# Causal attention: norms of the first batch made a stage earlier, and sums over keys for four heads every second slot

## The chip, the cores and the metric

The kernel runs on one core of a Trainium2 chip. The core has a matrix engine (TensorE, PE in the profile; its weight loads are listed as PEld), a vector engine (VectorE, DVE), an activation engine (ScalarE, ACT), a general engine (GpSimd, POOL) and queues for transfers (SyncE, SP, among them). The metric is the device time of one execution in microseconds. Before the change the median of three runs is 1987.32 us (1986.11 to 1991.52).

## The reference

The program is a stack of four layers over a tensor x of 4 batches, 512 tokens and 256 features in 32-bit floats. Each layer is an attention over a context of 64 tokens (for the second layer with an exponential feature map), and then a feed-forward part. The part that matters is that of the second layer: a causal attention with 16 heads of 16 features, queries and keys and values made from a latent, and then a mixture of experts.

```python
def rmsnorm(x, w):
    norm = jnp.sqrt(jnp.mean(x * x, axis=-1, keepdims=True)) + EPS
    return x / norm * w

def mla(xn, W_kvd, W_qd, W_ku, W_qu, W_vu, W_ropeq, W_ropek, W_o):
    kv_lat = xn @ W_kvd
    q_lat = xn @ W_qd
    ...                       # k, q: a plain and a rotated half; v
    scores = jnp.einsum('bqhd,bkhd->bhqk', qq, kk) * scale
    scores = jnp.where(causal[None, None], scores, jnp.finfo(scores.dtype).min)
    probs = jax.nn.softmax(scores, axis=-1)
    y = jnp.einsum('bhqk,bkhd->bqhd', probs, v).reshape(B, S, H)
    return y @ W_o
...
# the second layer
x = x + _L1_xattn_ref(ctx_1024, ctx_1024, _layernorm(x), ...)
x = _layernorm(x)             # inside the call of _L1_ffn_ref
x = x + mla(rmsnorm(x, w_ln1), ...)
x = x + moe(rmsnorm(x, w_ln2), ...)
```

So the causal attention of a batch starts with two norms of the same rows, one after the other: a layer norm, whose result is also the residual, and a root-mean-square norm.

## The kernel before

Tokens stand in blocks of 128 on the partitions; a batch is four such blocks. The stages that the change touches follow one another: the attention over the context of the second layer (`xattn`, in the profile from about 571 to 701 us), and the causal attention (`mla`, 701 to 1168). The mixture of experts comes after.

*The attention over the context* runs over four batches. For each it makes the queries of the next batch in between (the generator `new`, asked for a step by `some(new, n)` at five places), exponentials on ScalarE (`cpr`, L563), their sums over keys on TensorE (`ps_den`, L572), a reciprocal on VectorE (`crs`, L581), a broadcast of it (`ps_bc`, L591), the sums with the values (`ps_cy`, L597) and a projection (`ps_p`, L612). For the last batch `new` is empty.

*The causal attention* begins with `mla_heads` of batch 0, straight through: the layer norm into `xl` (ScalarE, L345), the squares (ScalarE, L354), a square root (L362), the multiplication into `xn` (VectorE, L368), transposes to `xnT` (TensorE, L377; copied out by VectorE, L381), and then the latent (`ps_lat`, L1180) and for each of four token blocks queries, values and keys (`ps_mq`, `ps_mv`, `ps_mk`), with copies on ScalarE (L1195, L1213), rotations on VectorE (L1186) and sums on GpSimd (L1196).

Then comes a loop over slots t = 0 to 140, with 128 slots of scores: four batches, four groups of four heads, four blocks of 128 queries or keys, two pairs of heads. Slot t does in TensorE's order:

- the scores of one pair of heads for the maximum (`ps_ms`, L1235), for 128 queries against all keys so far;
- the scores of the pair of slot t-11 for the weights (`ps_mx`, L1250), for 128 keys against all later queries, with the negative maximum as an extra feature. ScalarE takes the exponential (L1252) and GpSimd masks the diagonal block (L1254);
- the causal mask added to the first scores (L1238), which VectorE then reduces to the maximum (L1240);
- `behind(1)`: one piece of `mla_after` of the previous batch. These are, for each of four blocks, transposes of the sums (`ps_mn`), transposes back (`ps_myT`) and the projection (`ps_mw`), with VectorE's reciprocal, product and addition between them (L1310 for the addition); then the second norm and its transposes, the router (`ps_r`), the top two, the ranks (`ps_rank`), scatters of the rows on GpSimd's queue (`xs`, L859, eight a batch), and a shared expert (`ps_sg`, `ps_su`, `ps_sd`);
- the sums over keys of the pair of slot t-13 (`mla_sum`, `ps_mo`, L1273), 32 columns of the matrix engine for a head;
- in odd slots, `next(new)`: a piece of `mla_heads` of the next batch;
- when t%8 is 5, the transposes of queries and keys for the next group of heads (`mla_turned`, L1220); when t%8 is 2, at the start of the slot, those of the queries with their maxima.

TensorE takes its instructions in the order written (`in_order(PE)`); for the other engines a scheduler sets the order. In PSUM, the first scores have one buffer (`s1`, two banks for a pair of heads), so have the second (`s2`), and so has the output of the sums (`po`). The exponentials have four buffers (`mpr`). So the first scores of the next slot wait until VectorE has reduced those of this one.

```python
            behind(1)
            if last:
                self.mla_sum(pool, sts[last[0]], *last[1:], made.pop(last))
            ...
            if t % 2:
                next(new, None)
```

Of the kernel before, what the change touches and what calls it, by code (L numbers as in the profile page):

```python
# [11 lines left out]
F32 = mybir.dt.float32  # L12
# [10 lines left out]
P = 128  # L23
B, S, E = 4, 512, 256
# [164 lines left out]
class Net:  # L189
# [165 lines left out]
        return ss  # L355

    def rmsnorm(self, x, out):

        nc = self.nc
        ss = self.sumsq(x)  # L360
        nr = self.sm("rms_n", [P, GT])
        nc.scalar.activation(nr, ss, AF.Sqrt, scale=1.0 / E)  # L362
        ne = self.sm("rms_e", [P, GT])
        nc.vector.tensor_scalar(ne, nr, 1e-5, None, ALU.add)
        rs = self.sm("rms_r", [P, GT])
        nc.vector.reciprocal(rs, ne)
        for i in range(GT):
            nc.vector.tensor_scalar(out[:, i], x[:, i], rs[:, i : i + 1], None, ALU.mult)  # L368
# [265 lines left out]
        st.va = values(pool, g)  # L634
        yield

    def xattn(self, query, values, scale, dv, W, bias, before=None, after=None, keys=None, begin=lambda: None):

        with self.room("xattn") as pool, self.banks(mm=4, sc=1), ExitStack() as stack:
            mxs = [pool.tile([P, 4, 32], F32, tag=f"mx{i}", name=f"mx{i}", bufs=1) for i in range(GT)]
            for m in mxs:
                self.nc.gpsimd.memset(m, 0.0)
            for t in range(NT if before else 0):
                before.load(pool, t, self.nc.scalar if t // GT == 1 else self.nc.sync, bufs=12)
            stack.enter_context(self.in_order(PE))
            if keys:
                for _ in self.ctx_ready(pool, keys):  # L650
                    pass
            sts = [SimpleNamespace(g=g, pr=[]) for g in range(B)]
# [12 lines left out]

            nf = NH * dv // P
            old = late = iter(())
            new = heads(0)  # L670
            first = ExitStack()
            first.enter_context(self.in_order(ACT, DVE, POOL) if before else nullcontext())
            some(new)
            for st in sts:
                if st.g:
                    old = rest(sts[st.g - 1])
                new = heads(st.g + 1) if st.g + 1 < B else iter(())

# [24 lines left out]
            for _ in old:  # L703
                some(late, 1)
            some(late)
# [434 lines left out]
class Layers(Net):  # L1140


    def route(self, moe, g, rw, fine=False):
# [17 lines left out]

        return (whole for whole in steps() if whole or fine)

    def mla_heads(self, pool, g, st):


        nc = self.nc
        xl = st.xl = self.tail.tile([P, GT, E], F32, tag="xl", name="xl", bufs=3)
        self.layernorm(g, xl)
        yield  # L1170
        xr = self.xn_tile()
        self.rmsnorm(xl, xr)
# [89 lines left out]
        )  # L1262
        return pr

    def mla_sum(self, pool, st, o, j, h, pr):

        nc = self.nc
        if j == 0 and h == 0:
            st.po = self.po.tile([P, S], F32, name="ps_mo")
        for r in range(2):  # L1270
            n = 2 * h + r
            at = (4 * o + n) * (HD + 1)
            nc.tensor.matmul(  # L1273
                st.po[32 * n : 32 * n + 32, j * P :],
                st.va[:, j, at : at + 32],
                pr[:, r, : S - j * P],
                start=(j == 0),
                stop=(j == GT - 1),
                tile_position=(0, 32 * n),
            )  # L1280
# [57 lines left out]
        yield from moe.add(g, rows, *picked)  # L1338
        yield from self.shared_expert(pool, g, xT, sgu, sd)

    def mla(self, pool, short, tail, moe, sgu, sd, soon):

        nc = self.nc
        sts = [SimpleNamespace(qT={}, kT={}, qm={}, ys=[]) for _ in range(B)]
        for g, st in enumerate(sts):
            if g < 2:
                st.q, st.k = (  # L1350
                    (pool if g else short).tile([P, GT, NH, 32], F32, tag=f"m{n}{g}", name=f"m{n}{g}", bufs=1) for n in "qk"
# [33 lines left out]
        for t in range(32 * B + 13):  # L1385
# [27 lines left out]
            behind(1)  # L1413
        return old[0]

    def l1_ffn(self):
        nc, d = self.nc, self.d
        moe = Routed(self, 7, E, d["e1gu"], d["e1d"], "e1", STAMP, w=V_LN2)
        with ExitStack() as stack:
# [23 lines left out]
                moe.begin(stack.enter_context(self.room("l1h", side="right")))  # L1443

            with self.in_order(PE):
                last = self.mla(pool, short, tail, moe, sgu, sd, soon)
# [262 lines left out]
    def run(self):  # L1709
# [4 lines left out]

        W1, W3 = [], []
        moe = Routed(self, 8, 704, d["e0gu"], d["e0d"], "e0", 2 * STAMP)
        with ExitStack() as stack:
            with self.room("l0h") as held:
                with self.room("l0w", 1) as keep:
# [5 lines left out]
                with self.room("l0b", side="right") as pool, banks():  # L1725
# [8 lines left out]

                    with self.in_order(DVE, SP):
                        moe.blocks(pool, self.route(moe, B - 1, self.rw0, fine=True), other=later())
            self.xattn(
                self.query_features, self.values_features, 1.0 / 16.0, 2 * HD, W1[0], R_FCB, before=moe
            )
        moe = self.l1_ffn()  # L1740
        with banks():
            self.l2(moe)
        moe = Routed(self, 8, 512, d["e3gu"], d["e3d"], "e3", 0)
# [36 lines left out]
```

## Time and profile before

| what | us |
|---|---|
| median of the runs | 1987.32 (1986.11 to 1991.52) |
| the profiled execution's own time | 1997.2 |
| its span | 1995.5 |
| TensorE busy | 1712.2 (86%) |
| VectorE busy | 1020.4 (51%) |
| ScalarE busy | 671.4 (34%) |
| GpSimd busy | 424.3 (21%) |
| sums over keys, `ps_mo` L1273, 512 instructions | 97.1 |
| first scores, `ps_ms` L1235, 512 instructions | 111.7 |
| reductions, `mq` L1240, 128 instructions | 105.7 |
| first to last start of the first scores | 732.5 to 1133.2 |

A line of the timeline gives the start, the duration, the engine, the line of the kernel, the operation, the tiles (out <- in), the shape and the number of instructions put together, and in brackets how long the engine was idle before and what ended that. Of stretches, a line gives the length, the busy time of TensorE, its weight loads, VectorE, ScalarE and GpSimd with their number of instructions, the granted clock of TensorE as a share of full speed, the share of the transfer engines and the rate. A matrix product in 32-bit floats is two instructions in the profile, so the sum over keys of two heads shows as "x4".

### The profile page before, as it was taken

To read this page: it belongs to the slowest core of one execution; us is meant where nothing else is said; L and a number is where in the kernel's file an instruction comes from. 1 tells how busy PE (TensorE), PEld (TensorE's weight loads), DVE (VectorE), ACT (ScalarE), POOL (GpSimd) and SP (SyncE) were. 2 spreads that over 40 slices of the span, in tenths; PEclk is the share of its full clock that TensorE was granted. 3 is DMA by queue.
4 is the path that set the end of the run, shared out by engine and by line. 5 is a ranking of instruction groups with operands and counts; after the bars stand their busy time and mean duration, and the time that the engine had idled before them with its cause. 6 is when DMAs were issued, how large, how long until landed. Compare 5 with 4: busy or idle time off the path is not lost.

```text
span 1995.5 us, 25928 instructions
## 1 busy us (share of the span) xinstructions
PE 1712.2 (86%) x8752; PEld 970.5 (49%) x8752; DVE 1020.4 (51%) x3011; ACT 671.4 (34%) x1254; POOL 424.3 (21%) x594
## 2 busy tenths in 40 slices
PE   5878999999789868898989888985998887899993
PEld 2435666666444433343433344543665443455552
DVE  3655544444454343444454536546989565553333
ACT  3333222222254323335343432233445334222220
POOL 2031211111240021123131312223113103221112
PEclk8989999999899968998999999995899898999997
DMA  9528787887400100000001035972000001788884
GB/s 294 160 84 330 273 294 281 290 287 281 134 1 1 39 1 1 1 1 22 1 27 42 19 101 173 298 254 85 1 1 1 12 1 65 238 293 301 298 298 162
DMA packets 109350, 271.61 MB, mean 136 GB/s; under 512 B 13409, under 2 KB 71201, under 8 KB 99105
## 3 DMA queue, kind: packets, MB, share of 16 engines
q1 hardware_dynamic: 82976, 227.97, 33.9%
q0 software_dynamic: 10176, 28.00, 3.7%
q10 hardware_dynamic: 16064, 13.98, 2.1%
q8 instruction: 70, 1.15, 0.2%
q14 instruction: 64, 0.52, 0.1%
HBM read 220.48 MB, written 49.42 MB: 135 GB/s over the span
## 4 chain that ended last, share of the span: by engine, by line
PE 69%; DVE 18%; ACT 6%; issue 3%; DMA 2%; POOL 1%; SPq 0%; ACTq 0%; DVEq 0%; POOLq 0%
PE ps_gu L1030 20%; PE ps_de L1072 10%; PE ps_ms L1235 4%; PE ps_mo L1273 3%; DVE mq L1240 2%; PE ps_p L612 2%; PE ps_mx L1250 2%; PE ps_f L1633 2%; PE ps_xT L377 2%; PE ps_he L1059 2%; PE ps_bc L591 2%; ACT cpr L563 2%; PE ps_cx L557 1%; PE ps_ms L1238 1%; PE ps_cy L597 1%
## 5 line engine op out<-in xcount | busy, mean ns | idle before, releaser
L1030 PE MATMUL ps_gu<-e_wgu,e_xT 128*128 128x352 f32 (+1 forms) x1088 | 420.9, 526 | 13.1 <-DVE e_xT L1022 5.8
L1030 PEld LDWEIGHTS ps_gu<-e_wgu,e_xT 128*128 128x128 f32 x1088 | 195.5, 190 | 155.7 <-issue 71.4
L1072 PE MATMUL ps_de<-e_wd,e_hT 128*128 128x256 f32 x932 | 233.0, 387 | 10.8 <-ACT e_hT L303 3.1
L1075 POOL DMA_INDIRECT ys<-e_y,e_to x116 | 113.2, 976 | 482.6 <-ACT e_y L1074 336.5
L1072 PEld LDWEIGHTS ps_de<-e_wd,e_hT 128*128 128x128 f32 x932 | 172.8, 191 | 83.6 <-issue 39.0
L1047 DVE TENSOR_TENSOR e_h<-e_s,ps_gu 128x352 f32<-128x352 f32 (+2 forms) x155 | 83.4, 538 | 244.8 <-PE ps_gu L1030 185.0
L1240 DVE TENSOR_REDUCE mq<-ps_ms 128x2 f32<-128x256 f32 (+3 forms) x128 | 105.7, 826 | 139.9 <-PE ps_ms L1238 136.6
L1046 ACT ACTIVATE e_s<-ps_gu 128x352 f32<-128x352 f32 (+2 forms) x155 | 74.1, 478 | 280.3 <-PE ps_gu L1030 264.9
L1074 ACT ACTIVATE e_y<-ps_de,e_wt 128x256 f32<-128x256 f32 x116 | 55.0, 474 | 262.6 <-PE ps_de L1072 250.0
L1252 ACT ACTIVATE mpr<-ps_mx 128x1024 f32<-128x1024 f32 (+3 forms) x128 | 90.1, 704 | 146.9 <-PE ps_mx L1250 137.9
L1235 PE MATMUL ps_ms<-mkT,mqT 32*128 32x512 f32 (+3 forms) x512 | 111.7, 515 | 25.8 <-DVE mq L1240 24.3
L859 POOL DMA_INDIRECT xs<-xn,e_at x96 | 94.5, 985 | 120.4 <-DVE e_fi L893 39.7
L1250 PE MATMUL ps_mx<-mqm,mkT 32*128 32x128 f32 (+3 forms) x512 | 107.4, 497 | 1.3 <-ACT mpr L1252 1.3
L1254 POOL TENSOR_SCALAR_AFFINE_SELECT mpr<-mpr 128x256 f32<-128x256 f32 x128 | 52.2, 409 | 250.7 <-ACT mpr L1252 250.6
L1273 PE MATMUL ps_mo<-mpr,va 128*32 128x128 f32 (+3 forms) x512 | 97.1, 461 | 4.5 <-POOL mpr L1254 3.2
L1633 PE MATMUL ps_f<-w,xqT 128*128 128x352 f32 x256 | 86.1, 478 | 1.2 <-ACT xqT L1624 1.2
L1059 PE MATMUL ps_he<-consts_sb,e_h 128*128 128x128 f32 x466 | 76.3, 277 | 9.6 <-DVE e_h L1047 6.7
L557 PE MATMUL ps_cx<-q,kbd 32*128 32x512 f32 x256 | 45.2, 806 | 44.1 <-ACT cpr L563 44.1
L1235 PEld LDWEIGHTS ps_ms<-mkT,mqT 32*128 32x128 f32 x512 | 40.9, 195 | 80.6 <-DVE mq L1240 56.0
L1019 DVE COPY e_xT<-ps_xe 128x256 f32<-128x256 f32 x78 | 33.0, 423 | 86.7 <-PE ps_xe L1016 86.7
L377 PE MATMUL ps_xT<-consts_sb,xn 128*128 128x128 f32 x256 | 48.8, 330 | 32.4 <-ACT xn L345 18.7
L1059 PEld LDWEIGHTS ps_he<-consts_sb,e_h 128*128 128x128 f32 x466 | 53.7, 138 | 29.4 <-DVE e_h L1047 13.7
(317 smaller groups left out, 2816.0 us busy)
## 6 DMA issues: line engine op xcount, KB each, us to landing
e_wgu<-in_e0gu SPq DMA_DIRECT2D x39, 1408.0 KB
e_wgu<-in_e3gu SPq DMA_DIRECT2D x39, 1024.0 KB
e_wd<-in_e0d SPq DMA_DIRECT2D x39, 768.0 KB
e_wd<-in_e3d SPq DMA_DIRECT2D x39, 512.0 KB
e_wgu<-in_e1gu SPq DMA_DIRECT2D x38, 512.0 KB
xs<-z SPq DMA_DIRECT2D x16, 1040.0 KB
e_x<-xs SPq DMA_DIRECT2D x116, 130.0 KB
e_wd<-in_e1d SPq DMA_DIRECT2D x38, 256.0 KB
```

Of the source, the lines that this page charges most:

```text
L377: nc.tensor.transpose(ps[:, i * P : (i + 1) * P], x[:, i, c * P : (c + 1) * P], self.ident)
L859: r = nc.gpsimd.indirect_dma_start(out=net.xs, out_offset=bass.IndirectOffsetOnAxis(ap=at[:, k, i : i + 1], axis=0), in_=rows[:, i], in_of ...
L1030: nc.tensor.matmul(ps[:, :n], xT[:, c], wgu[:, c, cols], start=(c == 0), stop=(c == NC - 1))
L1059: self.nc.tensor.transpose(ps[:r, f - f0], h[:, f * P : f * P + r], net.ident)
L1072: nc.tensor.matmul(po[:, :E], hT[:r, f], wd[:r, f], start=(f == 0), stop=(f == self.nf - 1))
L1075: r = nc.gpsimd.indirect_dma_start(out=net.ys, out_offset=bass.IndirectOffsetOnAxis(ap=at, axis=0), in_=y, in_offset=None)
L1235: nc.tensor.matmul(ps[:, r, :n], st.qT[o][rows, diag], st.kT[o][rows, :n], start=True, stop=False)
L1240: nc.vector.tensor_reduce(st.q[:, i, at : at + 2, HD], ps[:, :, :n], AX.X, ALU.max, negate=True)
L1250: nc.tensor.matmul(ps[:, r, :n], st.kT[o][rows, keys], st.qm[o][rows, j * P :], start=True, stop=True)
L1252: nc.scalar.activation(pr[:, :, :n], ps[:, :, :n], AF.Exp, scale=HD**-0.5)
L1273: nc.tensor.matmul(st.po[32 * n : 32 * n + 32, j * P :], st.va[:, j, at : at + 32], pr[:, r, : S - j * P], start=(j == 0), stop=(j == GT - 1),
L1633: nc.tensor.matmul(ps[:, :H], xT[:, c], w[:, c, k * H : (k + 1) * H], start=(c == 0), stop=(c == NC - 1))
```

## The change

There are two parts.

*The norms of the first batch.* The layer norm, the root-mean-square norm and the transposes become a generator of their own, `mla_normed`. For batch 0 it is given to `xattn` of the second layer as `ahead`, in place of the empty `new` of its last batch, which takes a step from it at the places where the next batch's queries would be made. `xl` of batch 0 gets a buffer that outlives the stage. For the other batches `mla_heads` starts with `mla_normed`; it has one step more than before, so that the transposes and all that follow come one odd slot later.

*The slots.* `mla_sum` sums four heads at once, in even slots only, when the second pair of a group is ready. Pieces of the previous batch (`behind`) come twice in an odd slot, one before and one after the piece of the next batch, and not in even slots.

```diff
+    def rmsnorm_steps(self, x, out):
 
         nc = self.nc
         ss = self.sumsq(x)
         nr = self.sm("rms_n", [P, GT])
         nc.scalar.activation(nr, ss, AF.Sqrt, scale=1.0 / E)
+        yield
...
-                new = heads(st.g + 1) if st.g + 1 < B else iter(())
+                new = heads(st.g + 1) if st.g + 1 < B else iter(ahead)
...
+    def mla_normed(self, g, st):
+
+        xl, xr = st.xl, self.xn_tile()
+        yield from self.layernorm_steps(g, xl)
+        yield
+        yield from self.rmsnorm_steps(xl, xr)
+        yield
+        st.xT = self.transposed(xr, V_LN1)
+        yield
+
     def mla_heads(self, pool, g, st):
 
 
         nc = self.nc
-        xl = st.xl = self.tail.tile([P, GT, E], F32, tag="xl", name="xl", bufs=3)
-        self.layernorm(g, xl)
-        yield
-        xr = self.xn_tile()
-        self.rmsnorm(xl, xr)
-        yield
-        yield
-        xT = self.transposed(xr, V_LN1)
-        yield
+        if g:
+            yield from self.mla_normed(g, st)
+        xT = st.xT
...
-    def mla_sum(self, pool, st, o, j, h, pr):
-
-        nc = self.nc
-        if j == 0 and h == 0:
+    def mla_sum(self, pool, st, o, j, prs):
+
+        nc = self.nc
+        if j == 0:
             st.po = self.po.tile([P, S], F32, name="ps_mo")
-        for r in range(2):
-            n = 2 * h + r
+        for n in range(4):
             at = (4 * o + n) * (HD + 1)
             nc.tensor.matmul(
                 st.po[32 * n : 32 * n + 32, j * P :],
                 st.va[:, j, at : at + 32],
-                pr[:, r, : S - j * P],
+                prs[n // 2][:, n % 2, : S - j * P],
                 start=(j == 0),
                 stop=(j == GT - 1),
                 tile_position=(0, 32 * n),
             )
-        if j == GT - 1 and h == 1:
+        if j == GT - 1:
...
-            behind(1)
-            if last:
-                self.mla_sum(pool, sts[last[0]], *last[1:], made.pop(last))
+
+            if t % 2:
+                behind(1)
+            if last and last[3]:
+                g, o, j, _ = last
+                self.mla_sum(pool, sts[g], o, j, [made.pop((g, o, j, h)) for h in range(2)])
...
             if t % 2:
                 next(new, None)
+                behind(1)
...
             self.xattn(
-                self.query_features, self.values_features, 1.0 / 16.0, 2 * HD, W1[0], R_FCB, before=moe
+                self.query_features, self.values_features, 1.0 / 16.0, 2 * HD, W1[0], R_FCB,
+                before=moe, ahead=self.mla_normed(0, first),
             )
```

More of the change, by code (lines that the diff above doesn't have):

```diff
@@ L357, in rmsnorm @@
     def rmsnorm(self, x, out):
+        for _ in self.rmsnorm_steps(x, out):
+            pass
+    def rmsnorm_steps(self, x, out):
         nc = self.nc
@@ L635, in ctx_heads, with xattn @@
         yield
-    def xattn(self, query, values, scale, dv, W, bias, before=None, after=None, keys=None, begin=lambda: None):
+    def xattn(self, query, values, scale, dv, W, bias, before=None, after=None, keys=None, begin=lambda: None, ahead=()):
         with self.room("xattn") as pool, self.banks(mm=4, sc=1), ExitStack() as stack:
@@ L1339, in mla_after, with mla @@
         yield from self.shared_expert(pool, g, xT, sgu, sd)
-    def mla(self, pool, short, tail, moe, sgu, sd, soon):
+    def mla(self, pool, short, tail, moe, sgu, sd, first, soon):
         nc = self.nc
         sts = [SimpleNamespace(qT={}, kT={}, qm={}, ys=[]) for _ in range(B)]
+        sts[0].xl, sts[0].xT = first.xl, first.xT
         for g, st in enumerate(sts):
+            if g:
+                st.xl = tail.tile([P, GT, E], F32, tag=f"xl{g}", name=f"xl{g}", bufs=1) if g < 3 else first.xl
             if g < 2:
@@ L1414, in mla, with l1_ffn @@
         return old[0]
-    def l1_ffn(self):
+    def l1_ffn(self, first):
         nc, d = self.nc, self.d
@@ L1445, in l1_ffn @@
             with self.in_order(PE):
-                last = self.mla(pool, short, tail, moe, sgu, sd, soon)
+                last = self.mla(pool, short, tail, moe, sgu, sd, first, soon)
             mla.close()
@@ L1716, in run @@
         moe = Routed(self, 8, 704, d["e0gu"], d["e0d"], "e0", 2 * STAMP)
+        rows = ExitStack()
         with ExitStack() as stack:
@@ L1736, in run @@
                         moe.blocks(pool, self.route(moe, B - 1, self.rw0, fine=True), other=later())
+            first = SimpleNamespace()
+            first.xl = rows.enter_context(self.room("mla_first", 1)).tile([P, GT, E], F32, tag="xl", name="xl0")
             self.xattn(
-                self.query_features, self.values_features, 1.0 / 16.0, 2 * HD, W1[0], R_FCB, before=moe
-            )
-        moe = self.l1_ffn()
+                self.query_features, self.values_features, 1.0 / 16.0, 2 * HD, W1[0], R_FCB,
+                before=moe, ahead=self.mla_normed(0, first),
+            )
+        moe = self.l1_ffn(first)
+        rows.close()
         with banks():
```

## The prediction

> **What bounds the kernel now.** The page's table of engines has TensorE (PE) busy 86% of the span and VectorE 51%; its chain of waits is 69% PE and 18% VectorE. That is an average over stages, so I went to the stages touched: the end of the attention over the context (to 700.8 us) and the causal attention (701 to 1168), first by the timeline, then by stretches with their granted clock. This is PE at the seam between them (start, duration, line, operation, in brackets the idle time before and its releaser):
>
> ```profile
> 693.59 7.17 PE L612 MATMUL ps_p<-fcT_sb,cy 128*128 128x256 f32 x32
> 704.89 0.33 PE L377 MATMUL ps_xT<-consts_sb,xn 128*128 128x128 f32 x1 [4.12 <-DVE xn L368]
> ...
> 709.64 1.12 PE L377 MATMUL ps_xT<-consts_sb,xn 128*128 128x128 f32 x4 [0.84 <-DVE xnT L381]
> 710.55 3.62 PE L1180 MATMUL ps_lat<-xnT,Wlat_sb 128*128 128x512 f32 x4
> ```
>
> PE has nothing of its own from 700.76 to 710.55 but eight transposes, each late behind a normalization. Two more stretches of the timeline matter for where the norms go: the start of the last batch of the context attention, and its last reciprocal.
>
> ```profile
> 603.83 1.28 ACT L563 ACT_TABLE_LOAD   x1
> 605.13 1.88 ACT L563 ACTIVATE cpr<-ps_cx 128x2048 f32<-128x2048 f32 x1
> 607.06 2.00 PE L557 MATMUL ps_cx<-q,kbd 32*128 32x512 f32 x16 [0.54 <-ACT cpr L563]
> 611.91 1.07 PE L572 MATMUL ps_den<-cpr,pairs_sb 128*32 128x512 f32 x8 [1.00 <-ACT cpr L563]
> ```
>
> ```profile
> 680.32 3.36 DVE L581 RECIPROCAL crs<-ps_den 128x512 f32<-128x512 f32 x1 [10.89 <-PE ps_den L572]
> 683.74 1.24 PE L591 MATMUL ps_bc<-crs,pairs_sb 128*128 128x512 f32 x2 [3.48 <-DVE crs L581]
> ```
>
> In the first, PE waits for ScalarE's exponentials; in the second, it idles 3.48 us behind VectorE. In the causal attention the timeline shows the inside of a slot:
>
> ```profile
> 1029.27 0.28 PE L1238 MATMUL ps_ms<-caus,id 128*128 128x128 bf16 x2
> 1029.48 1.05 PE L1273 MATMUL ps_mo<-mpr,va 128*32 128x512 f32 x4
> 1029.59 1.23 DVE L1240 TENSOR_REDUCE mq<-ps_ms 128x2 f32<-128x1024 f32 x1
> 1030.87 0.70 PE L1235 MATMUL ps_ms<-mkT,mqT 32*128 32x512 f32 x2 [0.33 <-DVE mq L1240]
> ```
>
> The next slot's scores wait for the reduction of this one (one double buffer of scores), whatever PE did meanwhile. So a slot lasts its scores (ms, mx), then the longer of two: the reduction, or the other work on PE, its fill. With the durations of these rows, pitch = (ms+mx) + max(0.39 + reduction, 0.21 + fill). Last, the granted clock (stretch, length, busy us of PE, PEld, DVE, ACT, POOL, then PEclk, DMA):
>
> ```profile
> 732.50:741.00 8.50, 5.84 (x26) 3.02 (x28) 2.24 (x4) 0.00 (x0) 0.00 (x0) 0.50 0.00 0
> 831.40:834.80 3.40, 2.25 (x20) 1.05 (x22) 1.78 (x3) 1.63 (x2) 0.82 (x2) 1.00 0.00 0
> 834.80:838.20 3.40, 3.40 (x15) 0.58 (x8) 1.16 (x2) 0.81 (x1) 0.41 (x1) 0.50 0.00 0
> ```
>
> A stretch with PE busy 66% is followed by one at half clock.
>
> **Part 1, the norms of the first batch.** Removed from the seam: PE starts the latents (L1180) at 700.8 instead of 710.55, 9.8 us earlier. From there to the first scores (732.55) it is 22.0 us now. The chain in it is copies, rotations and POOL's sums (first at 717.0); ScalarE's eight normalizations (0.59 each) and eight squares (0.40) of batches 1 and 2, done now at 701 to 708 while PE waits, will stand among those copies, and POOL's sums behind its memsets, which begin when the last projection ends (700.83) and run to 708.4. Against that, half clock reigns now from 705.1 to 722.2, and PE comes straight from a full stretch of projections. So the way takes 19 to 22 us; the first scores come 9.8 to 13 us earlier, taken as 12.
>
> Added in the attention over the context: PE's eight transposes (0.48 each at half clock, 1.1 to 2.1 in all) go, in PE's written order, ahead of the broadcasts at 683.74, into the 3.48 us behind the reciprocal; their two copies (0.75 each) into 3.3 us in which VectorE idles after it. Cost nil; without that cover 2.1 us. But ScalarE's part goes between the norm's square root at 603.5 and the table load at 603.83: four normalizations (2.07), four squares and their sums (1.6), a square root (0.2), and about 0.6 of waiting for VectorE's 1/sd. Behind them are queued the exponentials of 605.13, which PE awaits 0.54 us already. So up to 4.5 us go straight onto the path; the lower bound is nil, if PE's weight work or later idle (1.00 before the L572 row) absorbs it. I take 4.5, as PE's order is fixed there. No DMA or SP instruction moves: the weights of the latents are issued by 695.6 and landed by 699. Head: -12 + 4.5 = **-7.5** (-13 to -3).
>
> **Part 2, sums of four heads.** Now each slot sums two heads: 1.05 us at 512 columns (0.98 on the path), less at fewer; 0.66 in the mean, 84.8 us over 128 slots. Four heads occupy four column groups. The nearest row is the denominators' (L572 above): eight instructions in 1.07 us against four in 1.05. So the four-head sum costs 0.08 more than the two-head one; the bounds are 0 and 0.98 (no overlap, which would leave nothing gained). Half the sums, 42 us of PE work, go. What they return is much less: an even slot keeps its reduction as floor, and an odd one falls to it.
>
> By the rule, slots 0 to 127 take 370.7 us before, and the trace has 401.5: most slots agree within 0.1, and the rest is half clock in slots 0 to 9 (+9.9) and stalls (+20.9). With the written order of after the rule gives 348.0. Two slots show the working. Slot 21 (number five of its eight, zero to seven): 0.86 + 0.21 + fill (sum 0.98, values 0.75, keys 0.87, turns 1.86) = 5.53, as measured; after: 0.86 + 0.21 + (queries 0.84, turns 1.86) = 3.77. Slot 27, number three: now 1.07 + 0.39 + 0.69 = 2.15, held by the reduction; after, values and keys (1.62) fall there: 2.90. Summed by number, zero to seven: -6.3, -0.3, -8.4, +13.6, -4.8, -12.3, -3.0, -1.2. Sum **-22.6**.
>
> Paired pieces make new stalls. Pieces of the previous batch go twice in an odd slot instead of once in each, so a piece follows its predecessor at once in PE's order: the transposes of a projected block wait for VectorE's reciprocal (0.2) and product (0.45). Where queries and keys do not lie between, that is 1.3 to 1.5 (slots 45, 77, 109), 0.8 to 1.3 at 113, 115 and 119, 0.25 at 47, 51, 79, 83. In slots 57 and 89 the second norm and its transposes share a slot: the squares, the table load (1.28), the root (0.2), the multiplications (1.14) make 5 to 5.5 us against 3.2 of PE work, so +2.2 each, and +3 at 121, where nothing fills. POOL's queue: eight row scatters per batch at 1.27 us pitch now go as two, six with a causal mask (L1254) between; after as three, three, two. The mask, and with it the sum, waits 3.8 us instead of 7.6; I price this at 2.3 a batch. Sum of these: 20. Of the 20.9 of stalls now, those at the scatter of slots 99 to 101 (7.5 over the rule) go or shrink, I take 8. Net **+12** (+4 to +20).
>
> The clock: where no pieces of a previous batch are left (slots 27 to 44, 59 to 66 and 91 to 98, 34 in all) the slots numbered six and seven of eight hold 3.2 us of PE work in 5.4, 60%, below the 66% that tripped at 831.4. A stretch at half clock costs 1.0 to 1.7 us; some eight more of them make **+9**. Bounds: nil, if windows straddle busier slots; +33, if all 34 run at half, at the price of 0.96 worked out below.
>
> Here the Trainium skill speaks against the change. "TensorE: Matmul & The Clock Gate" gives, under "Why this matters for your kernels", the rule that idle gaps of more than about 3 us are what to avoid if the clock is not to drop; by that this term would be nil. Under "A second HAM failure mode: psum-queue depth-cycling" it says that frequent micro-idles between groups of matmuls throttle too, which gives no price. The trace sides with the second: the longest idle in 831.4 to 834.8 was 0.71 us.
>
> The last slots (1134 to 1168, 34 us, PE busy 31.65) hold 13 two-head sums; half is 4.3 us, of which I take **-2** (-4 to 0), because masks behind six scatters still gate them.
>
> **Sum:** -7.5 - 22.6 + 12 + 9 - 2 = -11. It is made on the profiled execution (1997.2 us, 9.9 over the median of 1987.3); on the median it gives 1976.
>
> **Rivals.** *Slower, by the clock alone.* In slots 0 to 7, at half clock and without sums, the slots took 24.8 us where the rule gives 17.1: +0.96 a slot. Without the clock term the sum is -20; it turns at 21 extra slots at half clock and passes +6 at 27. All 34 quiet slots would give +33 - 20 = +13: 2000. For: return to full needs a stretch that is nearly all busy, and from 732 to 763 it did not come. Against: fills of 2.7 us or more every eight slots, at 834.8, returned it after one window. *More gained:* the clock stays full and the new stalls are hidden by the slack of even slots: -7.5 - 22.6 + 4 - 2 = -28, 1959. For: VectorE is free when its pieces come. Against: PE's order is written, so nothing passes a waiting piece. *Nothing to tell from before:* sums were hidden behind reductions anyway, the stalls and the clock eat the slots' gain (-22.6 + 20 + 9), and the head, half lost to the copies, is left at -5: with the tail at nil that is +1: 1989.
>
> **How the numbers follow.** The forecast with its terms near these (1968 to 1981) 0.34; more gained 0.20; same 0.16; slower 0.30. Faster: 0.34 + 0.20 = 0.54. About 0.3%, 6 us, is what a measurement tells from no change. The range, 1955 to 2003, leaves out the ends of the clock rival and of all terms at their best; the forecast's own is 1968 to 1981.
>
> **What would show it.** Right: L1180's matmuls start directly after the last projection; a gap of some 4 us ahead of the exponentials near 604 to 610; slots like 21 of 3.8 us; idle before the transposes of blocks in slots 45 and 57; four-head sums of 1.1 us at 512 columns. Wrong: four-head sums near 2 us (slots give nothing); granted clock of 0.5 over whole eights; the gap at 604 absent; or the masks' wait not shortened.

## The result, and the profile after

The changed kernel takes 2011.0 us (median of four runs, 2010.1 to 2014.0), the kernel before 1986.7 beside it: 1.0124 times as long, 95% interval 1.0098 to 1.0150. It is slower by 24 us where 11 us less were forecast, and the time lies outside the range of 1955 to 2003.

The two profiled executions differ by only 12.8 us, because that of before (1997.2) was 10 us above its median. Laid over one another by TensorE's instructions, they differ as follows: +5.2 us in the experts of the first layer, which the change does not touch; -5.4 between there and the first scores of the causal attention; +20.7 in the 128 slots; -2.1 in the last slots; -5.8 later, in the third and fourth layers, which the change does not touch either. So the head and the tail did about what was forecast, and the slots did the opposite. The three stages together give +13 us; where the other 11 us of the medians' difference lie, the two profiled executions do not show.

The page after, its first table and its chain of waits:

```profile
PE 1702.5 (85%) x8752; PEld 981.5 (49%) x8752; DVE 1015.8 (51%) x3011; ACT 670.2 (33%) x1254; POOL 422.4 (21%) x594
...
PE 69%; DVE 18%; ACT 6%; issue 3%; DMA 2%; POOL 1%; SPq 0%; ACTq 0%; DVEq 0%; POOLq 0%
```

In whole-span shares nothing is to be seen. The stretches show it: slots 0 to 126, then the ten slots from 57, then the ten from 89. The first three lines are of before, the other three of after (stretch, length, then busy us of PE, PEld, DVE, ACT, POOL, the granted clock, the transfers' share and rate):

```profile
732.55:1132.71 400.16, 354.22 (x2261) 153.93 (x2261) 183.50 (x381) 155.13 (x260) 83.93 (x174) 0.93 0.04 12
899.20:932.90 33.70, 29.43 (x193) 13.27 (x191) 17.87 (x56) 20.78 (x38) 6.79 (x13) 0.85 0.01 4
1010.95:1039.08 28.13, 24.87 (x195) 12.22 (x193) 16.57 (x52) 14.35 (x23) 7.12 (x14) 1.00 0.02 5
```

```profile
732.33:1152.49 420.16, 350.33 (x2260) 164.39 (x2260) 184.60 (x381) 154.86 (x260) 83.61 (x174) 0.83 0.04 11
896.19:937.28 41.09, 34.11 (x196) 17.12 (x193) 18.56 (x57) 20.86 (x38) 8.49 (x15) 0.63 0.03 10
1011.86:1055.10 43.24, 35.39 (x198) 18.27 (x195) 19.89 (x71) 14.55 (x23) 8.59 (x16) 0.64 0.03 10
```

TensorE lost about half of its time in the sums (`ps_mo` takes 55.2 us instead of 97.1) and its busy time fell by 4 us only, because it ran slower: the mean granted clock went from 0.93 to 0.83. In the ten slots from 57 and the ten from 89 it was 0.63 and 0.64, where it had been 0.85 and 1.00. Added up over the slots, TensorE was at half clock for 54.5 us before and for 141.9 us after.

The time of groups of slots, from the first scores of one to those of the next group, in us:

| slots | before | after | what lies there |
|---|---|---|---|
| 0-10 | 33.0 | 32.2 | no sums yet |
| 11-26 | 45.1 | 40.9 | heads of the next batch |
| 27-44 | 48.0 | 50.9 | little but scores and sums |
| 45-56 | 40.7 | 39.9 | projections of batch 0 |
| 57-66 | 33.7 | 41.1 | second norm, its transposes, router |
| 67-76 | 37.4 | 34.6 | scatters, shared expert |
| 77-88 | 40.7 | 40.0 | projections of batch 1 |
| 89-98 | 28.1 | 43.3 | second norm, its transposes, router |
| 99-108 | 39.2 | 31.7 | scatters, shared expert |
| 109-120 | 34.2 | 37.0 | projections of batch 2 |
| 121-126 | 20.2 | 28.7 | second norm, its transposes, router |

The three groups with a second norm lose 31 us, all others together gain 11. TensorE's timeline at the first of them, slot 57 of after:

```profile
895.41 0.85 PE L1281 MATMUL ps_mo<-mpr,va 128*32 128x384 f32 x8
896.19 0.49 PE L1244 MATMUL ps_ms<-mkT,mqT 32*128 32x128 f32 x4
899.09 0.80 PE L1259 MATMUL ps_mx<-mqm,mkT 32*128 32x128 f32 x4 [2.42 <-ACT mpr L1261]
899.82 0.39 PE L1247 MATMUL ps_ms<-caus,id 128*128 128x128 bf16 x2
900.01 1.59 PE L1212 MATMUL ps_mq<-Wup_sb,lat 128*128 128x384 f32 x2
```

And ScalarE's over the same stretch:

```profile
895.11 0.42 ACT L354 ACTIVATE sq<-xl 128x256 f32<-128x256 f32 x1 [1.88 <-DVE xl L1318]
...
895.63 1.28 ACT L366 ACT_TABLE_LOAD   x1
896.93 0.21 ACT L366 ACTIVATE rms_n<-ss 128x4 f32<-128x4 f32 x1
897.15 1.28 ACT L1261 ACT_TABLE_LOAD   x1
898.44 0.60 ACT L1261 ACTIVATE mpr<-ps_mx 128x512 f32<-128x512 f32 x1
```

The same place in the kernel before, TensorE and ScalarE (slot 57 starts at 899.20):

```profile
898.43 0.84 PE L1273 MATMUL ps_mo<-mpr,va 128*32 128x384 f32 x4
899.83 0.38 ACT L1252 ACTIVATE mpr<-ps_mx 128x256 f32<-128x256 f32 x1 [0.32 <-POOL x L1323]
899.86 0.63 PE L1273 MATMUL ps_mo<-mpr,va 128*32 128x256 f32 x4
900.24 1.28 ACT L362 ACT_TABLE_LOAD   x1
900.41 0.91 PE L1207 MATMUL ps_mv<-Wup_sb,lat 128*128 128x384 f32 x2
901.16 1.03 PE L1210 MATMUL ps_mk<-Wrk_sb,xnT 128*128 128x256 f32 x4
```

Three things are to be read. The first line of TensorE is a sum of four heads: eight instructions over 384 columns in 0.85 us, where four took 0.84 before; the sums do overlap. Then TensorE stands still for 2.42 us: the scores for the weights have one buffer, its last contents wait for an exponential, and that stands in ScalarE's order behind the norm's square root with a table load (1.28 us) on either side of it. Before, the exponential that TensorE needed next stood ahead of the table loads (899.83 against 900.24), and TensorE had a sum, values and keys to make meanwhile. The third is what follows: the queries of slot 57 take 1.59 us, where 0.91 is usual at full clock; half clock is granted from 897.9 to 915.0. Slot 57 takes 10.1 us instead of 3.4, slot 59 7.5 instead of 2.1. (Before, the transposes stood in slot 58; slots 57 and 58 together take 12.6 us instead of 7.2.)

At the seam, TensorE after:

```profile
706.52 7.17 PE L617 MATMUL ps_p<-fcT_sb,cy 128*128 128x256 f32 x32
713.53 1.88 PE L1189 MATMUL ps_lat<-xnT,Wlat_sb 128*128 128x512 f32 x4
716.09 0.91 PE L1212 MATMUL ps_mq<-Wup_sb,lat 128*128 128x384 f32 x2 [0.68 <-ACT lat L1190]
```

The latents follow the last projection at once and at full clock, 1.88 us instead of 3.62.

### The profile page after: what moved, and what is told of

The parts are those of the page before. It is cut to its first block, busy times and chain, and to the rows that moved or that the text cites. A ratio compares the mean times of both kernels' runs of the same rounds, so it can differ in the third digit from the quotient of the medians.

```text
span 2008.2 us, 25915 instructions
## 1 busy us (share of the span) xinstructions
PE 1702.5 (85%) x8752; PEld 981.5 (49%) x8752; DVE 1015.8 (51%) x3011; ACT 670.2 (33%) x1254; POOL 422.4 (21%) x594
## 4 chain that ended last, share of the span: by engine, by line
PE 69%; DVE 18%; ACT 6%; issue 3%; DMA 2%; POOL 1%; SPq 0%; ACTq 0%; DVEq 0%; POOLq 0%
PE ps_gu L1035 20%; PE ps_de L1077 10%; PE ps_ms L1244 5%; DVE mq L1249 3%; PE ps_mx L1259 2%; PE ps_p L617 2%; PE ps_xT L382 2%; PE ps_bc L596 2%; PE ps_f L1648 2%; PE ps_he L1064 2%; PE ps_ms L1247 2%; PE ps_cx L562 1%; PE ps_cy L602 1%; ACT cpr L568 1%; DVE mx L539 1%
## 5 line engine op out<-in xcount | busy, mean ns | idle before, releaser
L1244 PE MATMUL ps_ms<-mkT,mqT 32*128 32x512 f32 (+3 forms) x512 | 123.7, 564 | 32.7 <-DVE mq L1249 32.0
L1259 PE MATMUL ps_mx<-mqm,mkT 32*128 32x128 f32 (+3 forms) x512 | 120.5, 551 | 9.2 <-ACT mpr L1261 9.2
L382 PE MATMUL ps_xT<-consts_sb,xn 128*128 128x128 f32 x256 | 47.8, 334 | 25.4 <-ACT xn L345 20.1
L539 DVE TENSOR_REDUCE mx<-ps_cs 128x16 f32<-128x1024 f32 x48 | 56.8, 1217 | 12.8 <-PE ps_cs L531 12.8
```

The lines of the kernel that those rows point to most:

```text
L382: nc.tensor.transpose(ps[:, i * P : (i + 1) * P], x[:, i, c * P : (c + 1) * P], self.ident)
L1244: nc.tensor.matmul(ps[:, r, :n], st.qT[o][rows, diag], st.kT[o][rows, :n], start=True, stop=False)
L1259: nc.tensor.matmul(ps[:, r, :n], st.kT[o][rows, keys], st.qm[o][rows, j * P :], start=True, stop=True)
```

## The experiments

Two theories stood against each other at first. Theory A: the loss comes from the pieces of the previous batch in pairs. Theory B: it comes from the emptied slots as such, in which TensorE has too little work to keep its clock. Ratios are to the kernel before, run beside each experiment on the same chip (medians of 1988 to 1995 us there). "Half clock" is the sum over slots 0 to 126 of a profiled execution. The last column is for the whole program and is the mean of all executions: 2 x (1 - granted clock) x span, from the clock on record for each; the traces grant no other shares than 1 and 0.5.

| run | sums | pieces | ratio, 95% interval | slots 0-126, us | half clock, us | all executions, us |
|---|---|---|---|---|---|---|
| before | two heads | single | 1 | 400.2 | 54.5 | 275 to 282 |
| after | four | pairs | 1.0124 (1.0098 to 1.0150) | 420.2 | 141.9 | 376 |
| e1_norms | two | single | 1.0021 (1.0004 to 1.0039) | 413.2 | 81.9 | 289 |
| e2_sums | four | single | 0.9931 (0.9901 to 0.9960) | 394.0 | 112.4 | 333 |
| e3_pairs | two | pairs | 1.0236 (1.0200 to 1.0271) | 444.7 | 112.6 | 340 |
| e4_gap | four | pairs, gap | 1.0083 (1.0053 to 1.0113) | 418.6 | 129.7 | 360 |
| e5_sums_early | four | single | 0.9943 (0.9913 to 0.9972) | 386.9 | 91.7 | 332 |
| e6_norms_early | two | single | 1.0002 (0.9984 to 1.0019) | 398.4 | 47.8 | 282 |
| e7_fill | four | pairs | 1.0046 (1.0024 to 1.0069) | 410.3 | 106.5 | 334 |
| e8_single | four | pairs but five | 1.0242 (1.0215 to 1.0270) | 443.9 | 175.8 | 411 |
| e9_sums_fill | four | single | 0.9858 (0.9809 to 0.9908) | 389.5 | 89.1 | 295 |
| e10_after_fill | four | pairs | 0.9976 (0.9956 to 0.9997) | 399.9 | 78.5 | 297 |
| e11_before_fill | two | single | 0.9981 (0.9956 to 1.0006) | 397.2 | 47.8 | 278 |
| e12_sums_only | four | single | 0.9966 (0.9949 to 0.9983) | 389.9 | 105.8 | 336 |

### The two parts and the pairs, taken apart

e1_norms is the changed kernel with the sums and the pieces of before:

```diff
-            if t % 2:
-                behind(1)
-            if last and last[3]:
-                ...
+            behind(1)
+            if last:
+                self.mla_sum(pool, sts[last[0]], *last[1:], made.pop(last))
...
                 next(new, None)
-                behind(1)
```

> The first part alone: norms of the first batch in the attention over the context; sums of two heads in every slot and one piece of the previous batch in every slot, as before. Theory A (the paired pieces: the second norm and its transposes share a slot, TensorE waits there and the clock falls) and theory B (the emptied slots alone let the clock fall) both expect the head's gain and nothing else: 1987 - 5 = 1982, between 1977 and 1986. If it is slower than before, the head is a loss in itself.

It came out at 1.0021. The head's gain is in the trace, and the slots lose 13 us to those of before, which neither theory had: 6.3 of it in slots 27 to 44. There the additional step of `mla_normed` puts the eight transposes of batch 2 into slot 41, next to the four of the queries with their maxima, and the latents into slot 43, which then runs at half clock and takes 6.6 us. That execution (2003.9 us) was the slowest of its ten, whose median is 2001.1.

e2_sums is the changed kernel with only the pieces put back:

```diff
-            if t % 2:
-                behind(1)
+            behind(1)
             if last and last[3]:
...
                 next(new, None)
-                behind(1)
```

> The changed kernel with the pieces of the previous batch placed as before, one in every slot ahead of the sum; sums of four heads and the moved norms stay. Theory A: the losses at slots 57 to 65, 89 to 97 and 121 to 127 (30 us between the two traces) are gone and the sums' gain stays: 1962 to 1975, the pitch of slot 57 back near 3 us. Theory B: TensorE has as little work in its slots as in the changed kernel, so the clock falls as much: 1990 to 2010.

0.9931, faster than before: theory A's side. (Its 1962 to 1975 were reckoned from 1987 for the kernel before, of which 0.9931 is 1973; the median, 1982.9, was taken on a chip where the kernel before has 1994.9.) Slot 57 takes 1.8 us. But 112 us of half clock are left, twice those of before, so theory B holds for a part: the emptied slots bring half clock without any pair.

e3_pairs is the changed kernel with sums of two heads in every slot, and the pairs kept:

```diff
-            if last and last[3]:
-                g, o, j, _ = last
-                self.mla_sum(pool, sts[g], o, j, [made.pop((g, o, j, h)) for h in range(2)])
+            if last:
+                self.mla_sum(pool, sts[last[0]], *last[1:], made.pop(last))
```

> The changed kernel with sums of two heads in every slot as before, but the pieces of the previous batch in pairs in odd slots. Theory A: the waits of the pairs stay, so it is slower than before by 10 to 25 us: 1997 to 2012, with slots 57, 89 and 121 at 8 to 10 us. Theory B: no slot is emptied of its sum, so it is at 1980 to 1987.

1.0236, worse than even theory A had it; slots 57, 89 and 121 take 11.3, 10.0 and 9.1 us. With these the four combinations are complete (e1, e2, e3 and after, all with the norms moved). The pairs cost 1.0194 with four-head sums (1.0124 / 0.9931) and 1.0215 with two-head ones; the four-head sums gain 0.9910 with single pieces and 0.9891 with pairs. So the sums are a gain of about 1% in either place, and the pairs a loss of about 2%. In the traces the pairs cost 26 and 32 us of slots. Both parts bring half clock: over all executions the pairs 43 and 51 us, the four-head sums 44 and 36.

### What it is in a pair that costs

e4_gap moves the transposes of the second norm one slot pair away from it:

```diff
             nc.gpsimd.tensor_tensor(x, x, xl[:, i], ALU.add)
         yield
+        yield
         xT = self.transposed(xr, V_LN2)
```

> The changed kernel with one empty piece more between the second norm of a batch and its transposes, so that the transposes come a slot pair later. Theory A: slots 57, 89 and 121 fall from 8.7 to 10.1 us to about 3 and most of the half clock behind them goes: 15 to 28 us less than the changed kernel, 1983 to 1996. Theory B: at most 3 us less, 2008 to 2011.

1.0083, some 8 us less than the changed kernel's ratio, which is about half of theory A's least (the intervals overlap). Slot 57 still takes 6.2 us, since what waits there first is not a transpose but the scores behind ScalarE's table loads; slots 57 to 66 and 89 to 98 fall by 12 us, and slots 67 to 76 and 99 to 108, with the scatters, rise by 13. So the distance of norm and transposes is not what costs at slot 57.

e8_single keeps the pairs, but takes the five pieces from the second norm to the router's choice singly:

```diff
+            one = 12 <= pieces < 17
-            if t % 2:
+            if t % 2 or one:
                 behind(1)
...
                 next(new, None)
-                behind(1)
+                if not one:
+                    behind(1)
```

> The changed kernel with pieces of the previous batch in pairs in odd slots, except for the five from the second norm to the router's choice, which come singly in every slot as before. If the pair of norm and transposes is the loss, slots 57 to 66, 89 to 98 and 121 to 126 fall from 113 us to 85 to 92 (82 before) and the kernel is 20 to 28 us faster than the changed one, near 1.000 of before. If pairs cost wherever they wait, as the run with the gap suggests, at most 10 us.

1.0242: 12 parts in a thousand slower than the changed kernel, where a gain was expected. The edit did not restore the place of before. There the norm's piece came in slot 57, and a sum, values and keys stood between it and its transposes; here it comes in slot 56, and the transposes stand first in slot 57, ahead of the queries. Slots 57 to 66 take 50.2 us, and half clock rises to 175.8. The wait of 2.42 us for ScalarE is there as in the changed kernel. So a piece being alone is not enough; that what counts is how much of TensorE's other work stands between a piece and the one that needs its result is a reading of this trace, and was not tested by itself.

### The clock against the wait

e7_fill gives TensorE useless work into the very wait, and shortens no wait:

```diff
+            if t in (57, 89, 121):
+                ps = self.tr.tile([P, S], F32, tag="tr", name="ps_fill")
+                for _ in range(3):
+                    nc.tensor.matmul(ps, self.ident, self.Wup[:, :S], start=True, stop=True)
             if then:
                 made[then] = self.mla_weights(pool, sts[then[0]], *then[1:])
```

> The changed kernel with three additional 512-column products, whose result nobody reads, in TensorE's order of slots 57, 89 and 121, ahead of the scores that wait there 2.4 us for ScalarE; the wait hides 2.7 us of work. Theory of the clock (the idle time at these slots throttles, and the half clock after it is most of the loss): full clock stays on behind slots 57, 89 and 121, 8 to 18 us less than the changed kernel. Theory of the wait itself: no gain, 0 to 3 us more.

1.0046 against 1.0124: the changed kernel gets about 15 us (0.8%) faster by doing nine more products. Half clock falls by 35 us, the slots by 9.9. Slot 57 does not become shorter than the wait allows (8.0 us), and slot 59 is at half clock still, but slot 91 takes 4.6 us instead of 8.7, and slot 123 3.0 instead of 5.7. The profiled execution (1994.8 us) was the fastest of its six; over all six, half clock is 42 us less than in the changed kernel (334 against 376).

On top of e7_fill, e10_after_fill adds a product of 64 to 352 columns in each slot in which TensorE only waits for the reduction:

```diff
+            if t in FILL:             # a number of columns for each of 41 slots
+                ps = self.tr.tile([P, S], F32, tag="tr", name="ps_fill")
+                nc.tensor.matmul(ps[:, : FILL[t]], self.ident, self.Wup[:, : FILL[t]], start=True, stop=True)
             if last == (B - 2, 3, GT - 1, 1):
                 soon()
```

> The changed kernel with the same fill in the slots in which its TensorE only waits (42 slots), and the three products ahead of the waiting scores of slots 57, 89 and 121 as in e7_fill. Theory of the clock: half clock in slots 0 to 126 falls from 142 us to 60 to 90 and the kernel is 20 to 30 us faster than the changed one, 0.997 to 1.002 of before. If the waits themselves are the loss: as e7_fill at best, 1.004 or more.

0.9976 against 1.0124: 29 us back, with the waits of the pairs all in place (slot 57 takes 8.0 us, as in e7_fill). The stretches of its slots 0 to 126, 57 to 66 and 89 to 98:

```profile
727.07:1126.96 399.89, 355.97 (x2360) 169.26 (x2360) 184.11 (x381) 154.33 (x260) 83.55 (x174) 0.90 0.04 12
884.15:919.32 35.17, 29.54 (x204) 14.42 (x200) 18.36 (x57) 20.44 (x38) 8.01 (x15) 0.90 0.04 12
993.79:1033.30 39.51, 35.55 (x208) 16.95 (x204) 20.37 (x74) 14.56 (x23) 10.05 (x17) 0.73 0.05 17
```

The clock of slots 57 to 66 is 0.90 where it was 0.63, and the ten slots take 35.2 us instead of 41.1, with 8 instructions more. Slots 89 to 98 gain less: 0.73 where it was 0.64, 39.5 us instead of 43.2. A product that nobody reads cannot shorten a wait for another engine, so this, with the control that follows, shows that the clock is the larger part of the loss: half clock is down by 63 us and the slots by 20.3, 0.32 us for each us of half clock.

e11_before_fill puts the same kind of fill (31 slots) into the kernel before, with the diff of e10_after_fill and its own columns.

> The kernel before with the same kind of fill (31 slots). It has 54 us of half clock in slots 0 to 126, 31 of them in slots 0 to 10, which are the same in all kernels. Theory of the clock: 5 to 10 us faster, 0.995 to 0.997 of before; it tells how much of the gain of the filled kernels has nothing to do with the change. Otherwise 1.000 to 1.002.

0.9981, with an interval that takes in 1. Half clock falls from 54.5 to 47.8 only, and the 31 us of slots 0 to 10 do not go: the fill makes TensorE 92% busy there (25.17 of 27.30 us; 77% without), and full clock does not come sooner. So the gain of the fill in the changed kernel is not one that any kernel would have.

### The parts by themselves, and a faster version

e6_norms_early and e5_sums_early are e1_norms and e2_sums without the additional step, so that batches 1 to 3 have their transposes where they were:

```diff
         if g:
-            yield from self.mla_normed(g, st)
+            self.layernorm(g, st.xl)
+            yield
+            xr = self.xn_tile()
+            self.rmsnorm(st.xl, xr)
+            yield
+            yield
+            st.xT = self.transposed(xr, V_LN1)
+            yield
```

> As e1_norms (norms of batch 0 moved, sums and pieces as before), without the additional step for batches 1 to 3: the move alone. The traces put the first scores 5.3 us earlier against the start of the stage, and the slots are those of before: 0.997 of before (0.996 to 0.998), slots 27 to 44 back from 54.3 to 48 us. If the order of heads isn't the cause of what e1_norms lost in the slots (13 us), it stays at 1.002.

Slots 27 to 44 are back at 46.4 us, so in the traces the additional step was what e1_norms lost there. How much it costs in the mean is less certain: this profiled execution was the fastest of its ten, and the intervals of the two ratios overlap. The move alone is at 1.0002; the expected 0.997 lies outside the interval. In its trace the first scores do come 5.2 us earlier than before, measured from the experts of the first layer. It was to be more: at the seam alone it is 13 us. Some 2 us are lost ahead of the norms, from 545 to 606 us, in part to a window of half clock (578.9 to 582.3) that the kernel before does not have. Most of the rest is lost where the norms went, in TensorE's timeline of this run:

```profile
606.50 1.98 PE L516 MATMUL ps_qf<-xnT,fw_sb 128*128 128x512 f32 x4
613.37 3.48 PE L562 MATMUL ps_cx<-q,kbd 32*128 32x512 f32 x16 [4.89 <-ACT cpr L568]
616.69 0.60 PE L566 MATMUL ps_cx<-mT,pairs_sb 32*128 32x512 f32 x4
```

The wait for ScalarE is 4.89 us instead of 0.54, and the products that follow take 3.48 us instead of 2.00: one window of half clock, from 613.0 to 616.4, follows on this wait too. The shift against before jumps from +1.97 to +7.81 us there.

> As e2_sums (sums of four heads, one piece of the previous batch in every slot, norms of batch 0 moved), but for batches 1 to 3 the transposes, latents, queries, keys and values come as early as before the change (one odd slot earlier; mla_normed's additional step is left out). If the later step is what lets the clock fall in slots 27 to 44 (54.1 us in e2_sums, 47.9 before), they fall to 46 to 49 and the kernel is 5 to 8 us faster than e2_sums: 0.988 to 0.991 of before. If the emptied slots do it, slots 27 to 44 stay at 52 to 54 and the ratio at 0.993.

Slots 27 to 44 fall from 54.1 to 44.2, more than expected, but the median of the ratio does not move against e2_sums (0.9943 and 0.9931, intervals overlap): in its trace slots 57 to 66 and 89 to 98 take 8 us more.

e12_sums_only is the kernel before with the sums of four heads and nothing else.

```diff
-            if last:
-                self.mla_sum(pool, sts[last[0]], *last[1:], made.pop(last))
+            if last and last[3]:
+                g, o, j, _ = last
+                self.mla_sum(pool, sts[g], o, j, [made.pop((g, o, j, h)) for h in range(2)])
```

> The kernel before with one edit: sums of four heads, in even slots. Norms of the first batch and pieces of the previous batch stay where they were. If the gain of e5_sums_early (0.9943) is that of the sums, and the moved norms give nothing that can be told (e6_norms_early, 1.0002), it is at 0.993 to 0.996. If the 5 us that the traces show for the moved norms are real, it is at 0.996 to 0.999. In its trace the first scores start at the place of before, and slots 0 to 126 take 385 to 392 us.

0.9966, a gain of 7 us, and 389.9 us of slots, with half clock up from 54.5 us to 105.8: the sums alone nearly double it, and the kernel is faster all the same. It lies in the upper of the two ranges, which speaks for a moved norm worth some 5 us in e5_sums_early (0.9943); the intervals overlap, so that is not settled.

e9_sums_fill is e5_sums_early with the fill in 29 slots, and one product of 512 columns in slots 58, 90 and 122 in the manner of e7_fill.

> As e5_sums_early, with a product of 64 to 352 columns that nobody reads at the end of each slot in which TensorE otherwise only waits for the reduction (30 slots, each filled to half its idle time, so that it would fit at half clock too), and one of 512 columns in slots 58, 90 and 122 ahead of the scores that wait for ScalarE. TensorE gets more work and no wait gets shorter. Theory of the clock: half clock in slots 0 to 126 falls from 92 us to below 60, and the kernel is 6 to 15 us faster than e5_sums_early: 0.986 to 0.991 of before. If idle time doesn't set the clock: no gain, 0.994 to 0.997.

0.9858, 0.9809 to 0.9908: the fastest of all, 28 us less than before, and faster than both kernels. The two profiled executions do not show why: half clock is 89.1 us against 91.7 without fill, not below 60. But that execution (1976 us) was the slowest of its four, and that of e5_sums_early (1973 us) the second fastest of its eight. The clock on record for every execution shows the fall: 295 us of half clock in the mean against 332, with granted clocks of 0.922 to 0.930 against 0.906 to 0.923. In the group of slots 27 to 44 the trace has no half clock left, slots 121 to 126 take 3 us more.

## Why the prediction was wrong, point by point

**The head (-7.5) was right in kind and near in size.** The seam gave 13 us where 12 were forecast. Against that stood 4.5 for ScalarE's part ahead of the exponentials: the wait grew by 4.35, as written, but the half-clock window after it made the step 5.8. The net in the trace is -5.4; of what is missing, some 2 us went ahead of the norms, and up to 0.9 at the transposes, which were priced at nil. That no gain can be told from e6_norms_early (1.0002) says that it may be smaller still.

**The sums (-22.6) were right as work, at full clock.** Four heads cost 0.01 us more than two at 384 columns (0.08 was taken), and where no clock and no wait interfered the rule for a slot held: slot 21 takes 3.54 us (3.77 forecast), slot 27 2.85 (2.90). The four combinations put the sums at -0.9 to -1.1%, 18 to 22 us, but in the kernel before (e12_sums_only) they give 7 us only. Both are net of half clock that the sums bring: in e12_sums_only the slots fall by 10.3 us while half clock rises by 51, which at 0.32 us each is 16; without it, the sums would be worth some 27. The prediction had this price in another term, the clock.

**The waits of the pairs (+12 net) were near in size as waits.** In e7_fill they stand at almost full clock: the slots 57 and 58, 89 and 90, 121 and 122 take 29.3 us there, 21.9 before and 36.4 in the changed kernel. So the waits of the second norm come to 7.3 us, where 2.2 + 2.2 + 3 were forecast. For all waits there is only a remainder: with the rule's -22.6 and a price of 0.32 us for each us of half clock, the 87 us more of half clock are 28 us; the slots came to +20, so 20 + 22.6 - 28 = 15 us are left. This is worked out, not measured by itself.

**The clock (+9) is the term that failed: 28 us.** The step was "some eight more" stretches at half clock. The price of a stretch was right (0.32 x 3.41 = 1.1 us, at the lower end of 1.0 to 1.7); their number was not: 87 us are 26 stretches of 3.41 us. The prediction counted them from what the quiet slots hold for themselves. Half of the 87 us did come in the 34 slots that it named (13.7 in slots 27 to 44, 9.7 in 59 to 66, 20.2 in 91 to 98), which is 13 stretches and not eight; the other half came in slots 57, 58, 89, 90 and 121 to 126, which it had priced as waits, at +2.2, +2.2 and +3, as if the clock stayed full. Windows of 3.41 us in which TensorE was busy 63, 52 and 32% were followed there by 17, 31 and 27 us of half clock, and the three groups of slots lost 31 us. So the two terms were summed as if they had nothing to do with each other, where the waits set off half clock that then lies over the quiet slots behind them. The waits are not the whole of it: in slots 45 to 126, half clock is 20.5 us before, 51.0 and 58.0 with four-head sums and single pieces (e2_sums, e12_sums_only), and 90.7 in the changed kernel. So 30 to 37 of these 70 us come with the emptied slots alone, and the rest with the pairs. The sign of being wrong that the prediction named, a granted clock of 0.5 over whole eights, is what the trace has from 1014.0 to 1044.7.

**The rival "slower, by the clock alone"** had the right sign, about the right price (0.96 for a slot) and half of the place. Its ceiling for the clock, +33 us, holds (28), and so does its +13 in all, for the two profiled executions (+12.8); the medians lie 11 us further apart, which these executions do not place, and so the kernel came out above its 2000 us.

**The POOL queue** went in the order that was forecast, three, three and two scatters with a mask between them, but the masks' wait did not fall to 3.8 us: the longest from an exponential to its mask is 7.3 us instead of 7.8 in batch 1, and 6.1 instead of 7.8 in batch 0. Slots 99 to 108 gain 7.5 us; that they had 6.8 us of half clock before and have none now is a part of it.

**The page that was weighed.** "TensorE: Matmul & The Clock Gate" of the Trainium skill, under "Why this matters for your kernels", warns of idle gaps above about 3 us. The trace sides against it more clearly than before: at slot 57 one gap of 2.42 us, 1.3 of it in the window that half clock followed, was enough. Its statement under "What's actually happening" that one busy window of 3.4 us brings full clock back agrees with the length of the pieces (3.4 us, and multiples of it), but not as a rule: full clock came back after 58 of 93 windows that were at least 95% busy, and 35 such windows brought nothing; the numbers are below.

## What to carry to other kernels

A wait on TensorE has two prices: its own length, and the half clock that it can set off, which ended here almost only after a stretch that was filled nearly without a gap. Where a schedule removes work from TensorE's slots, look first for the slots that will wait for a chain on another engine (here a norm with two table loads on ScalarE), keep other work between the piece that starts the chain and the piece that needs it, and price the clock at those places as well as in the quiet ones. Three useless products in each of three waits made this kernel 0.8% faster: a cheap test of whether it is the clock.

## What the runs showed of the hardware that was not expected

The clock is granted in windows of 3.41 us, and going down and coming back have different conditions. Cutting the stretch from 690 to about 1170 us, the causal attention, of six traces (before, after, e1 to e4) into such windows, and counting what followed a window by the share in which TensorE was busy:

| busy share of the window | at full clock: half clock follows | at half clock: full clock follows |
|---|---|---|
| below 0.50 | 21 of 22 | 0 of 2 |
| 0.50 to 0.60 | 21 of 36 | 0 of 7 |
| 0.60 to 0.75 | 9 of 68 | 0 of 36 |
| 0.75 to 0.95 | 6 of 288 | 3 of 66 |
| 0.95 and above | 2 of 229 | 58 of 93 |

So a stretch that is 60 to 90% busy mostly keeps whichever clock it has: it seldom falls by itself, and once it has fallen it hardly comes back by itself. That fits with one bad slot in 32 being worth 17 to 31 us of half clock. What sets apart the 35 windows at half clock that were nearly full and yet brought nothing is open.
